# A graph-network layer on one core: the first and the second matmul layer of an edge group in two alternating halves

## The chip, the core and the metric

The kernel runs on one core of a Trainium2 chip. The core has a matrix engine (TensorE; PE in the profile, with its weight loads as PEld), a vector engine (DVE), a scalar engine (ACT), a general engine (POOL), an engine that issues transfers (SP), and 16 DMA engines. The metric is the device time of one execution in microseconds. A group of numbers such as 128x256 is partitions by elements.

## The reference

There are 6250 nodes with 128 features and 100000 edges, sorted by destination. The part that takes the time is the edge network, whose messages are summed by destination:

```python
row, col = (edge_index[0], edge_index[1])
msg_in = jnp.concatenate([node_features[row], node_features[col]], axis=-1)
h = jax.nn.relu(msg_in @ Wm1 + bm1)
h = jax.nn.relu(h @ Wm2 + bm2)
messages = h @ Wm3 + bm3
agg = jax.ops.segment_sum(messages, col, num_segments=num_nodes)
count = jax.ops.segment_sum(jnp.ones((messages.shape[0],), messages.dtype), col, num_segments=num_nodes)
agg = agg / jnp.clip(count, 1.0)[:, None]
node_in = jnp.concatenate([node_features, agg], axis=-1)
upd = jax.nn.relu(node_in @ Wn1 + bn1) @ Wn2 + bn2
return node_features + upd
```

Outside it, the result is `_layernorm(x + that)`. Hidden width is 256, so a hidden vector is two chunks of 128 (`HC = 2`).

## The kernel before, in words

**Tables.** `Wm1` is split into its half for the source and its half for the destination. A first stage computes a table `atab` with one row of 256 numbers in f32 for each node (the source's share of the first layer), and a table `btab` with the destination's share, each number as three bf16 terms. Later blocks of `btab` are made inside the edge loop (L663, then `b_terms`).

**The edge loop.** Edges go in 196 groups of 512 (`NG`, `GT = 4` tiles of 128 edges). The source rows of a group are gathered from `atab` by four indirect DMAs of 128 rows each, issued by POOL (L455), into one buffer `rows`, of which a pool holds four. The destination terms of a group come by two DMAs (groups 0 to 107, `nk` = 1) or four (groups 108 to 195, `nk` = 2) that SP issues (L466), into `terms`, six buffers. Then for group g:

- `first_layer` builds the first layer's sums in one PSUM tile `ph` of two banks, one bank for each half of the partitions (`h`), and both chunks `c` in each bank. Sixteen transposes (L509) bring the gathered rows into it; bf16 matmuls (L516), four of 256 columns with `nk` = 1 and eight of 128 columns with `nk` = 2, add the destination's terms. Two ACT instructions of 128x512 (L521) add the bias, apply relu, and write `h1` in SBUF.
- `second_layer` of group g-1 follows: for two pairs of tiles, a PSUM bank with four f32 matmuls of 256 columns (each is two matmul instructions in the profile, so eight a bank and sixteen a group, L530); one DVE instruction of 128x512 (L532) a bank takes it to `h2`.
- Before the second layer, in some groups, `sums` (L542) adds up edges by destination with one-hot matmuls, ACT copies the result (L550), and at the start of the next group TensorE turns it (L561) and DVE adds it to the totals (L571). Up to group 83 four groups are added at a time, then two, and from group 160 on one.

The first six groups (`XS = 3`) gather from `x` itself and use a matmul (L504) in place of the transposes.

**Order.** TensorE, ACT and DVE run in the order in which the program is written (the manual schedule). In an iteration that is on TensorE: turning of old sums, `first_layer(g)`, sums, `second_layer(g - 1)`, and sometimes a block of `btab`. POOL and SP keep a planner's order; their instructions wait for semaphores. A `rows` buffer comes free when all sixteen transposes that read it are done; the gathers of group g+4 wait for that. There are two `ph` tiles, so a group's first layer may begin while the previous group's is still being read.

**After the loop** a node stage of some 100 us computes the update and the layer norm. A further loop over groups with a wide range of destinations (L694) stands in the program and calls the same two functions, with a run-time count.

Of the kernel before, what the change touches and what calls it, by code (L numbers as in the profile page):

```python
# [33 lines left out]
def kernel(  # L34
# [181 lines left out]
            nc.sync.dma_start(btab[n0:n0 + (i + m) * P].rearrange("(p i) c h -> p i c h", p=P), bt[:, :i + m])  # L216

    edge = ExitStack()
    ld = edge.enter_context(tc.tile_pool(name="ld", bufs=4, side="right"))

    with tc.tile_pool(name="prep", bufs=1) as prep, tc.tile_pool(name="pp", bufs=3, space=PSUM) as pp, tc.tile_pool(
        name="pb", bufs=5, space=PSUM
# [181 lines left out]
        b_block = None  # L404
        for i in range(BLOCKS):
            tiles = range(4 * i, min(4 * i + 4, NT), 2)
            rows = ld.tile([P, GT, H], F32, name="rows")
# [29 lines left out]
    with edge, tc.tile_pool(name="wk", bufs=2) as wk, tc.tile_pool(  # L437
# [8 lines left out]
        def bank():  # L446
            return p2.tile([P, 2, H], F32, name="bank")
# [1 line left out]
        def flat_bank():  # L449
            return bank().rearrange("p t h -> p (t h)")  # L450

        def gather(idx):
            ag = ld.tile([P, GT, H], F32, name="rows")
            for j in range(GT):
                nc.gpsimd.indirect_dma_start(  # L455
                    out=ag[:, j, :], out_offset=None, in_=atab[:, :],
                    in_offset=bass.IndirectOffsetOnAxis(ap=idx[:, j:j + 1], axis=0))
            return ag
# [3 lines left out]
        def fetch(firsts, nk):  # L462
            bw = ld.tile([P, 2, H], BF16, name="terms", bufs=6)
            for j in range(0, len(firsts), 2 // nk):
                terms = btab[ds(firsts[j], WB + 1)].rearrange("n c h -> (n c) h")
                nc.sync.dma_start(bw[halves[j // 2], j % 2, :], terms[:NQ])  # L466
            return bw
# [27 lines left out]
            (nc.scalar.copy if g % 2 else nc.vector.tensor_copy)(xt, px)  # L495
            return xt

        def first_layer(ag, bw, oht, nt, nk, xt=None):
            nh = nt // 2
            ph = p1.tile([P, 2, HC, HE], F32, name="ph")  # L500
            for c in range(HC):
                if xt is not None:
                    for h in range(nh):
                        nc.tensor.matmul(ph[:, h, c, :], w1[:, 0, c * P:(c + 1) * P], xt[:, h * HE:(h + 1) * HE],  # L504
                                         start=(c == 0), stop=False, skip_group_check=True)
                    continue
                for u in range(GT):
                    for h in range(nh):
                        nc.tensor.matmul(ph[:, h, c, u * NQ:(u + 1) * NQ], ag[halves[h], u, c * P:(c + 1) * P],  # L509
                                         ident[halves[h], halves[h]], is_transpose=True,  # L510
                                         start=(c == 0 and u == 0), stop=False, skip_group_check=True)
            n = HE // nk
            for c in range(HC):
                for k in range(nk):
                    for h in range(nh):
                        nc.tensor.matmul(ph[:, h, c, k * n:(k + 1) * n], bw[halves[h], k, c * P:(c + 1) * P],  # L516
                                         oht[halves[h], k * n:(k + 1) * n], start=False, stop=True,
                                         skip_group_check=True)
            h1 = wk.tile([P, HC, GE], F32, name="h1", bufs=3)
            for c in range(HC):  # L520
                nc.scalar.activation(h1[:, c, :nh * HE].rearrange("p (h e) -> p h e", h=nh), ph[:, :nh, c, :],  # L521
                                     AF.Relu, bias=b1[:, c:c + 1])
            return h1

        def second_layer(h1, h2, nt):
            for j0 in range(0, nt, 2):
                ph2 = bank()
                for j in range(j0, j0 + 2):
                    for c in range(HC):
                        nc.tensor.matmul(ph2[:, j - j0, :], h1[:, c, j * P:(j + 1) * P],  # L530
                                         w2[:, c, :], start=(c == 0), stop=(c == HC - 1))
                nc.vector.tensor_tensor(h2[:, j0:j0 + 2, :H], ph2, nb2.to_broadcast([P, 2, H]), op=ALU.max)  # L532

        def sums(banks):

# [48 lines left out]
        def nk_of(g):  # L584
            return 1 if g < 2 * HALVES else 2
# [33 lines left out]
        for i in range(NG + 2 + WAIT + 1):  # L619
# [10 lines left out]
            if i < NG:  # L630
                bw = fetch(load_bases(tilei[0:1, i * GT:(i + 1) * GT], NTS[i], ENG.SP), nk_of(i))
                if i % 4 == 0 and i + 4 < NG:
                    rels[i // 4 + 1] = places(i // 4 + 1)
                st[i] = dict(bw=bw, ag=gather(srcT[:, i, :]) if i >= 2 * XS else None)
            g = i - 2
            if g < 0:
                continue
# [4 lines left out]
                turning = None  # L642
            if g < NG:
                s = st[g]
                s["h1"] = first_layer(s.pop("ag"), s.pop("bw"), ohts[g // 2][:, g % 2], NTS[g], nk_of(g),
                                      xts.pop(g, None))
                if g + 1 < 2 * XS:
                    xts[g + 1] = x_turn(g + 1)
                if g % 2 == 0 and g + 2 < NG:
                    make_hot(g // 2 + 1)  # L650
            if g in jobs:
                gs = jobs.pop(g)
                units_now = [w for k in gs for w in units_of(k)]
# [40 lines left out]
        with tc.For_i(0, groups, 1) as g:  # L694
            more = nc.values_load(
                morei[0:1, ds(g, 1)], min_val=0, max_val=N // 16,
                skip_runtime_bounds_check_because="the difference of two nodes over 16")
            dcol = wk.tile([P, GT], I32, name="dcol", bufs=1)
            bcol = wk.tile([P, GT], F32, name="bcol", bufs=1)
            dl = wk.tile([P, GT], F32, name="dl", bufs=1)  # L700
            db = wk.tile([P, HE], I32, name="db", bufs=1)
            with nc.allow_non_contiguous_dma(reason="a destination a partition"):
                nc.sync.dma_start(dcol, dpad[ds(g * GE, GE)].rearrange("(j p) -> p j", p=P))
            for h, half in enumerate(halves):
                nc.sync.dma_start(db[half], dpad_row[:, ds(g * GE + h * HE, HE)].to_broadcast([NQ, HE]))
            nc.sync.dma_start(bcol, basetab.rearrange("(o t) -> o t", o=1)[:, ds(g * GT, GT)].to_broadcast([P, GT]))
            nc.vector.tensor_sub(dl, dcol, bcol)
            with tc.For_i(0, more, 1):
                idx = wk.tile([P, GT], I32, name="idx")
                nc.vector.tensor_copy(idx, srcT[:, ds(g, 1), :].rearrange("p o j -> p (o j)"))  # L710
                pbc = wk.tile([P, 2], F32, name="pbc")
                for h, half in enumerate(halves):
                    nc.vector.tensor_scalar(pbc[half], bcol[half, 2 * h:2 * h + 2], iota_p[half], None, op0=ALU.add)

                ti = wk.tile([1, GT], I32, name="ti")
                nc.vector.tensor_scalar_min(ti, tilei[0:1, ds(g * GT, GT)], float(N - 1))
                ag, bw = gather(idx), fetch(load_bases(ti, GT, ENG.SP), 2)
# [5 lines left out]
                h1 = first_layer(ag, bw, oht[:, 0], GT, 2)  # L723
                second_layer(h1, h2s[0], GT)
# [186 lines left out]
```

## Time and profile before

| | |
|---|---|
| median of 3 runs | 1420.95 us (1420.75 to 1423.0) |
| the profiled execution | 1419.83 us, span 1418.1 us |
| TensorE busy | 1254.4 us, 88% of the span, 10152 matmuls |
| POOL busy | 766.0 us, 54% (760 gathers in the edge loop) |
| DVE busy | 535.5 us, 38% |
| ACT busy | 374.8 us, 26% |
| DMA | 165.66 MB, 117 GB/s on average |
| mean granted TensorE clock | 0.968 of full |

How to read it. In the list of groups a row gives line, engine, operation, what is written and read, its shape, how often, then busy time and the mean of one, then the idle time just before these instructions and what ended it. "issue" there means that the engine waited for nothing that the profile shows. In the timeline a row gives the start, the time from the first start to the last end of the merged instructions, the engine, the line, the operation, the count, and in brackets the idle time before it. A matmul's stated duration is longer than the step from one to the next, as they are pipelined: steps are read from starts. Instruction counts in the text count a weight load and a matmul as two.

### The profile page before, as it was taken

Reading aid. Unit: us, or ns where it says so; the run is one execution under the profiler, and the core shown is the slowest. Engines: PE = TensorE matmul, PEld = TensorE weight load, DVE = VectorE, ACT = ScalarE, POOL = GpSimd, SP = SyncE. Lnnn points to the kernel's source line nnn. Section 1 sums busy time; section 2 is a strip of 40 time slices with the busy share of each in tenths; the row PEclk is TensorE's granted clock in tenths of the full one; section 3 lists DMA queues with packets and bytes.
Section 4 is the critical chain, followed back from the end, with each engine's and each line's share of the span. In section 5 each row is a group of like instructions: output and inputs, shape, how many; then the busy total and the mean of one; then the engine's idle time right before and its main releaser. Section 6 shows DMA issues by size and latency. Waiting matters only on the chain. (4 is left out here: it accounts for less than half of the span.)

```text
span 1418.1 us, 27156 instructions
## 1 busy us (share of the span) xinstructions
PE 1254.4 (88%) x10152; PEld 921.6 (65%) x10153; DVE 535.5 (38%) x1289; ACT 374.8 (26%) x674; POOL 766.0 (54%) x810
## 2 busy tenths in 40 slices
PE   4689899898988988898988888998989889999997
PEld 3566676676666766676766666676666666667555
DVE  2533333333333423333333333333333344444554
ACT  1442222222222222222222122222222222222234
POOL 6125566565665655656656566566666656652210
PEclk8789999999999999999999999999999999999999
DMA  6533244344344434434334443444444444441422
GB/s 220 201 92 106 80 146 127 96 135 124 115 120 119 126 103 126 130 99 140 111 111 115 118 119 113 123 116 120 113 119 119 113 123 113 113 114 31 114 79 74
DMA packets 106276, 165.66 MB, mean 117 GB/s; under 512 B 26443, under 2 KB 66633, under 8 KB 106125
## 3 DMA queue, kind: packets, MB, share of 16 engines
q0 software_dynamic: 37248, 101.24, 25.7%
q1 hardware_dynamic: 68349, 62.39, 14.2%
q8 instruction: 81, 1.33, 0.4%
q14 instruction: 54, 0.44, 0.1%
q10 hardware_dynamic: 544, 0.26, 0.1%
HBM read 144.27 MB, written 19.89 MB: 116 GB/s over the span
## 5 line engine op out<-in xcount | busy, mean ns | idle before, releaser
L455 POOL DMA_INDIRECT rows<-atab,srcT x760 | 723.5, 952 | 528.5 <-PE ph L516 228.3
L530 PE MATMUL bank<-w,h 128*128 128x256 f32 x3128 | 746.1, 390 | 11.0 <-issue 8.8
L530 PEld LDWEIGHTS bank<-w,h 128*128 128x128 f32 x3128 | 585.8, 193 | 154.2 <-issue 64.2
L521 ACT ACTIVATE h<-ph,b 128x512 f32<-128x512 f32 x392 | 247.3, 682 | 733.8 <-PE ph L516 419.0
L532 DVE TENSOR_TENSOR x_sb<-bank,nb 128x512 f32<-128x512 f32 x313 | 214.3, 691 | 568.5 <-PE bank L530 224.1
L542 PE MATMUL bank<-x_sb,oh 128*32 128x257 f32 x1252 | 135.4, 402 | 22.7 <-issue 21.7
L516 PE MATMUL ph<-oht,terms 64*128 64x128 bf16 (+1 forms) x1132 | 97.0, 240 | 52.8 <-issue 45.4
L509 PE MATMUL ph<-ident,rows 64*128 64x64 f32 x3032 | 133.2, 227 | 3.3 <-issue 3.3
L509 PEld LDWEIGHTS ph<-ident,rows 64*128 64x128 f32 x3032 | 111.2, 139 | 36.0 <-issue 36.0
L532 DVE TENSOR_TENSOR h_more<-bank,nb 128x512 f32<-128x512 f32 x78 | 53.4, 691 | 148.6 <-PE bank L530 70.1
L571 DVE TENSOR_TENSOR acc<-acc,bank 128x96 f32 x378 | 96.1, 254 | 23.0 <-PE ph L516 2.4
L542 PEld LDWEIGHTS bank<-x_sb,oh 128*32 128x32 f32 x1252 | 51.6, 112 | 70.1 <-issue 53.9
L516 PEld LDWEIGHTS <-terms 64*128 64x128 bf16 x1132 | 46.9, 97 | 69.9 <-issue 62.3
L542 PE MATMUL bank<-h_more,oh 128*32 128x257 f32 x312 | 63.0, 407 | 5.1 <-issue 4.7
L550 ACT COPY part<-bank 128x257 f32<-128x257 f32 (+1 forms) x95 | 35.6, 374 | 110.0 <-PE bank L530 59.3
L792 POOL TENSOR_TENSOR agg<-agg,rc 128x512 f32<-128x512 f32 (+2 forms) x15 | 18.5, 1238 | 85.2 <-DVE agg L790 45.6
L561 PEld LDWEIGHTS bank<-ident,part 64*128 64x128 f32 x567 | 25.1, 138 | 55.0 <-ACT part L550 27.6
L561 PE MATMUL bank<-ident,part 64*128 64x64 f32 x567 | 38.3, 240 | 22.5 <-ACT part L550 21.5
L370 PE MATMUL pbt<-w,xT 128*128 128x256 f32 x114 | 32.1, 430 | 18.4 <-ACT xT L389 10.8
L484 DVE TENSOR_TENSOR oh<-iota_n,dloc 128x256 f32<-128x256 f32 x98 | 41.0, 418 | 0.0
L370 PEld LDWEIGHTS pbt<-w,xT 128*128 128x128 f32 x114 | 23.3, 217 | 22.7 <-ACT xT L389 11.6
L479 DVE TENSOR_SCALAR oht<-places,iota_p 128x512 bf16<-128x512 bf16 x98 | 33.7, 344 | 0.0
(138 smaller groups left out, 537.0 us busy)
## 6 DMA issues: line engine op xcount, KB each, us to landing
terms<-btab SPq DMA_DIRECT2D x566, 32.0 KB
places<-reltab SPq DMA_DIRECT2D x98, 128.0 KB
rows<-atab,srcT POOLq DMA_INDIRECT x760
btab<-x_sb SPq DMA_DIRECT2D x10, 768.0 KB
atab<-rows SPq DMA_DIRECT2D x12, 512.0 KB
x_sb<-in_x_dram SPq DMA_DIRECT2D x5, 512.0 KB
xr<-in_x_dram SPq DMA_DIRECT2D x10, 256.0 KB
rc<-rtab SPq DMA_DIRECT2D x10, 256.0 KB
```

Source lines behind the costliest of these rows:

```text
L370: nc.tensor.matmul(pbt[:, a, :], xT[:, (t0 + a) * P:(t0 + a + 1) * P], w1[:, k, :], start=True, stop=True)
L455: nc.gpsimd.indirect_dma_start(out=ag[:, j, :], out_offset=None, in_=atab[:, :], in_offset=bass.IndirectOffsetOnAxis(ap=idx[:, j:j + 1], a ...
L484: nc.vector.tensor_tensor(oh[:, :ng].rearrange("p g j n -> p (g j) n"), iota.to_broadcast([P, ng * GT, WN]), dl.rearrange("p (j o) -> p j ...
L509: nc.tensor.matmul(ph[:, h, c, u * NQ:(u + 1) * NQ], ag[halves[h], u, c * P:(c + 1) * P], ident[halves[h], halves[h]], is_transpose=True, ...
L516: nc.tensor.matmul(ph[:, h, c, k * n:(k + 1) * n], bw[halves[h], k, c * P:(c + 1) * P], oht[halves[h], k * n:(k + 1) * n], start=False, st ...
L521: nc.scalar.activation(h1[:, c, :nh * HE].rearrange("p (h e) -> p h e", h=nh), ph[:, :nh, c, :], AF.Relu, bias=b1[:, c:c + 1])
L530: nc.tensor.matmul(ph2[:, j - j0, :], h1[:, c, j * P:(j + 1) * P], w2[:, c, :], start=(c == 0), stop=(c == HC - 1))
L532: nc.vector.tensor_tensor(h2[:, j0:j0 + 2, :H], ph2, nb2.to_broadcast([P, 2, H]), op=ALU.max)
L542: nc.tensor.matmul(pg[w * WN:(w + 1) * WN, :H + 1], oh, h2, start=(t == 0), stop=(t == len(tiles) - 1), skip_group_check=True)
L550: nc.scalar.copy(part[:nt * WN, i], pg[:nt * WN, :H + 1])
L561: nc.tensor.matmul(pts[h][:, i, c, :], rows, ident[halves[h], halves[h]], is_transpose=True, start=True, stop=True, skip_group_check=True)
L571: nc.vector.tensor_add(window, window, pts[h][:, i, :, k:k + WN])
```

## The change

A group's first layer is cut in two halves `s` = 0, 1. Half 0 transposes the rows of gathers 0 and 1, half 1 those of gathers 2 and 3; each adds its destination terms and has ACT instructions of its own, on 128x256 in place of 128x512. Every half has four bf16 matmuls of 128 columns, for both values of `nk`. The second layer is cut by edge tiles in the same way (tiles 0 and 2, then 1 and 3; one PSUM bank and one DVE instruction each, as before). In an iteration TensorE now runs: turning of old sums, first layer of g half 0, sums, second layer of g-1 half 0, first layer of g half 1, second layer of g-1 half 1. The four `rows` buffers are one tile, addressed by `g % 4`, so that a gather waits for the readers of its own part. The wide loop's calls change along.

```diff
-    ld = edge.enter_context(tc.tile_pool(name="ld", bufs=4, side="right"))
+    ld = edge.enter_context(tc.tile_pool(name="ld", bufs=1, side="right"))
+    rows_of_groups = ld.tile([P, 4, GT, H], F32, name="rows")
...
-        def gather(idx):
-            ag = ld.tile([P, GT, H], F32, name="rows")
+        def gather(g, idx):
+            ag = rows_of_groups[:, g % 4]
...
-        def first_layer(ag, bw, oht, nt, nk, xt=None):
+        def first_layer(part, s):
+
+            ag, bw, oht, nt, nk, xt = part["of"]
             nh = nt // 2
-            ph = p1.tile([P, 2, HC, HE], F32, name="ph")
+            if s == 0:
+                part["ph"] = p1.tile([P, 2, HC, HE], F32, name="ph")
+                part["h1"] = wk.tile([P, HC, GE], F32, name="h1", bufs=3)
+            ph, h1 = part["ph"], part["h1"]
             for c in range(HC):
...
-                for u in range(GT):
+                for u in (2 * s, 2 * s + 1):
                     for h in range(nh):
...
-            n = HE // nk
+            k = s if nk == 2 else 0
             for c in range(HC):
-                for k in range(nk):
-                    for h in range(nh):
-                        nc.tensor.matmul(ph[:, h, c, k * n:(k + 1) * n], bw[halves[h], k, c * P:(c + 1) * P],
-                                         oht[halves[h], k * n:(k + 1) * n], start=False, stop=True,
-                                         skip_group_check=True)
-            h1 = wk.tile([P, HC, GE], F32, name="h1", bufs=3)
+                for h in range(nh):
+                    nc.tensor.matmul(ph[:, h, c, s * P:(s + 1) * P], bw[halves[h], k, c * P:(c + 1) * P],
+                                     oht[halves[h], s * P:(s + 1) * P], start=False, stop=True,
+                                     skip_group_check=True)
             for c in range(HC):
-                nc.scalar.activation(h1[:, c, :nh * HE].rearrange("p (h e) -> p h e", h=nh), ph[:, :nh, c, :],
-                                     AF.Relu, bias=b1[:, c:c + 1])
-            return h1
+                nc.scalar.activation(h1[:, c, :].rearrange("p (h s e) -> p h s e", h=2, s=2)[:, :nh, s],
+                                     ph[:, :nh, c, s * P:(s + 1) * P], AF.Relu, bias=b1[:, c:c + 1])
...
+        def second_layer(h1, h2, nt, s):
+            js = range(s, nt, 2)
+            ph2 = bank()
+            for i, j in enumerate(js):
+                for c in range(HC):
+                    nc.tensor.matmul(ph2[:, i, :], h1[:, c, j * P:(j + 1) * P],
+                                     w2[:, c, :], start=(c == 0), stop=(c == HC - 1))
+            m = len(js)
+            nc.vector.tensor_tensor(h2[:, s:s + 2 * m - 1:2, :H], ph2[:, :m], nb2.to_broadcast([P, m, H]), op=ALU.max)
...
-                s["h1"] = first_layer(s.pop("ag"), s.pop("bw"), ohts[g // 2][:, g % 2], NTS[g], nk_of(g),
-                                      xts.pop(g, None))
+                s["of"] = s.pop("ag"), s.pop("bw"), ohts[g // 2][:, g % 2], NTS[g], nk_of(g), xts.pop(g, None)
+                first_layer(s, 0)
...
-            if 0 <= g - 1 < NG:
-                second_layer(st.pop(g - 1)["h1"], h2s[(g - 1) % len(h2s)], NTS[g - 1])
+            for half in range(2):
+                if half and g < NG:
+                    first_layer(st[g], 1)
+                if 0 <= g - 1 < NG:
+                    second_layer(st[g - 1]["h1"], h2s[(g - 1) % len(h2s)], NTS[g - 1], half)
+            st.pop(g - 1, None)
```

More of the change, by code (lines that the diff above doesn't have):

```diff
@@ L406 @@
             tiles = range(4 * i, min(4 * i + 4, NT), 2)
-            rows = ld.tile([P, GT, H], F32, name="rows")
+            rows = rows_of_groups[:, i % 4]
             for n, t0 in enumerate(tiles):
@@ L496, in x_turn @@
             return xt
-        def first_layer(ag, bw, oht, nt, nk, xt=None):
+        def first_layer(part, s):
+            ag, bw, oht, nt, nk, xt = part["of"]
             nh = nt // 2
-            ph = p1.tile([P, 2, HC, HE], F32, name="ph")
+            if s == 0:
+                part["ph"] = p1.tile([P, 2, HC, HE], F32, name="ph")
+                part["h1"] = wk.tile([P, HC, GE], F32, name="h1", bufs=3)
+            ph, h1 = part["ph"], part["h1"]
             for c in range(HC):
                 if xt is not None:
-                    for h in range(nh):
+                    for h in range(nh if s == 0 else 0):
                         nc.tensor.matmul(ph[:, h, c, :], w1[:, 0, c * P:(c + 1) * P], xt[:, h * HE:(h + 1) * HE],
@@ L511, in first_layer @@
                                          start=(c == 0 and u == 0), stop=False, skip_group_check=True)
-            n = HE // nk
+            k = s if nk == 2 else 0
             for c in range(HC):
-                for k in range(nk):
-                    for h in range(nh):
-                        nc.tensor.matmul(ph[:, h, c, k * n:(k + 1) * n], bw[halves[h], k, c * P:(c + 1) * P],
-                                         oht[halves[h], k * n:(k + 1) * n], start=False, stop=True,
-                                         skip_group_check=True)
-            h1 = wk.tile([P, HC, GE], F32, name="h1", bufs=3)
-            for c in range(HC):
-                nc.scalar.activation(h1[:, c, :nh * HE].rearrange("p (h e) -> p h e", h=nh), ph[:, :nh, c, :],
-                                     AF.Relu, bias=b1[:, c:c + 1])
-            return h1
[L525 to L532, printed above, removed]
+                for h in range(nh):
+                    nc.tensor.matmul(ph[:, h, c, s * P:(s + 1) * P], bw[halves[h], k, c * P:(c + 1) * P],
+                                     oht[halves[h], s * P:(s + 1) * P], start=False, stop=True,
+                                     skip_group_check=True)
+            for c in range(HC):
+                nc.scalar.activation(h1[:, c, :].rearrange("p (h s e) -> p h s e", h=2, s=2)[:, :nh, s],
[9 more added lines that the diff above has]
+            nc.vector.tensor_tensor(h2[:, s:s + 2 * m - 1:2, :H], ph2[:, :m], nb2.to_broadcast([P, m, H]), op=ALU.max)
         def sums(banks):
@@ L633 @@
                     rels[i // 4 + 1] = places(i // 4 + 1)
-                st[i] = dict(bw=bw, ag=gather(srcT[:, i, :]) if i >= 2 * XS else None)
+                st[i] = dict(bw=bw, ag=gather(i, srcT[:, i, :]) if i >= 2 * XS else None)
             g = i - 2
@@ L716 @@
                 nc.vector.tensor_scalar_min(ti, tilei[0:1, ds(g * GT, GT)], float(N - 1))
-                ag, bw = gather(idx), fetch(load_bases(ti, GT, ENG.SP), 2)
+                ag, bw = gather(0, idx), fetch(load_bases(ti, GT, ENG.SP), 2)
                 oht = wk.tile([P, 2, HE], BF16, name="oht")
@@ L722 @@
                 oh = hot_nodes(dl, 1, iota_b)
-                h1 = first_layer(ag, bw, oht[:, 0], GT, 2)
-                second_layer(h1, h2s[0], GT)
+                wide = dict(of=(ag, bw, oht[:, 0], GT, 2, None))
+                for half in range(2):
+                    first_layer(wide, half)
+                for half in range(2):
+                    second_layer(wide["h1"], h2s[0], GT, half)
                 part = part_of(sums([[[(oh[:, 0, j, :], h2s[0][:, j, :])] for j in range(GT)]]), [GT])
```

## The prediction, made before the result was known

> **What bounds the kernel now.** I read the page first, then busy time by stage, then the timeline of TensorE in groups with and without idle time, then the waits.
>
> The page's busy times, and three stretches of the loop (columns: stretch, its length, busy time and count of PE, PEld, DVE, ACT and POOL, granted clock, DMA share, GB/s):
>
> ```profile
> PE 1254.4 (88%) x10152; PEld 921.6 (65%) x10153; DVE 535.5 (38%) x1289; ACT 374.8 (26%) x674; POOL 766.0 (54%) x810
> ```
> ```profile
> 618.00:1098.00 480.00, 432.61 (x3856) 320.18 (x3854) 171.71 (x402) 114.22 (x199) 293.60 (x310) 0.99 0.42 118
> 1098.00:1275.00 177.00, 159.38 (x1542) 117.18 (x1540) 72.78 (x192) 42.93 (x84) 107.20 (x114) 1.00 0.41 115
> 1286.00:1303.00 17.00, 17.00 (x186) 12.95 (x180) 8.66 (x24) 4.95 (x10) 0.63 (x1) 1.00 0.08 17
> ```
>
> TensorE is the bound, yet in most of the loop it idles for a tenth; at 1286 to 1303, when gathers and destination terms are over (DMA share 0.08), it does not idle at all. The same groups with and without idle time:
>
> ```profile
> 1161.62 0.66 PE L509 MATMUL ph<-ident,rows 64*128 64x64 f32 x16
> 1162.12 0.57 PE L516 MATMUL ph<-oht,terms 64*128 64x128 bf16 x4
> 1163.20 0.29 PE L516 MATMUL ph<-oht,terms 64*128 64x128 bf16 x4 [0.51 <-issue]
> ...
> 1167.88 0.66 PE L509 MATMUL ph<-ident,rows 64*128 64x64 f32 x16
> ```
> ```profile
> 1285.91 0.66 PE L509 MATMUL ph<-ident,rows 64*128 64x64 f32 x16
> 1286.41 0.39 PE L516 MATMUL ph<-oht,terms 64*128 64x128 bf16 x8
> 1286.73 0.64 PE L542 MATMUL bank<-h_more,oh 128*32 128x257 f32 x8
> ...
> 1291.18 0.66 PE L509 MATMUL ph<-ident,rows 64*128 64x64 f32 x16
> ...
> 1296.45 0.66 PE L509 MATMUL ph<-ident,rows 64*128 64x64 f32 x16
> ```
>
> A group takes 6.26 us (1161.62 to 1167.88) or 5.27 (1285.91 to 1291.18). The lost microsecond lies inside the bf16 matmuls, at the end of a run of small instructions, and waits for nothing that the profile shows. In the waits of TensorE such "issue" leads:
>
> ```profile
> PE ph L516 <- issue: 45.4, 74, 1.5
> PE bank L542 <- issue: 26.4, 53, 1.1
> PE bank L561 <- ACT part L550: 21.5, 12, 5.0
> ```
>
> What the loop loses in all comes from paces. Starts of the transposes, from group 6 on, with groups of a full pace between them:
>
> ```profile
> 113.58 0.71 PE L509 MATMUL ph<-ident,rows 64*128 64x64 f32 x16
> ...
> 120.20 0.66 PE L509 MATMUL ph<-ident,rows 64*128 64x64 f32 x16
> ...
> 403.90 0.66 PE L509 MATMUL ph<-ident,rows 64*128 64x64 f32 x16
> ...
> 409.23 0.71 PE L509 MATMUL ph<-ident,rows 64*128 64x64 f32 x16
> ...
> 413.74 0.71 PE L509 MATMUL ph<-ident,rows 64*128 64x64 f32 x16
> ...
> 623.68 0.71 PE L509 MATMUL ph<-ident,rows 64*128 64x64 f32 x16
> ...
> 906.66 0.66 PE L509 MATMUL ph<-ident,rows 64*128 64x64 f32 x16
> 911.13 0.71 PE L509 MATMUL ph<-ident,rows 64*128 64x64 f32 x16
> ...
> 926.17 0.71 PE L509 MATMUL ph<-ident,rows 64*128 64x64 f32 x16
> ...
> 931.92 0.66 PE L509 MATMUL ph<-ident,rows 64*128 64x64 f32 x16
> ...
> 1098.27 0.71 PE L509 MATMUL ph<-ident,rows 64*128 64x64 f32 x16
> ```
>
> Groups 6 to 85 go in fours: one with sums, 6.62 (113.58 to 120.20), one with a block of `btab`, 5.33 (403.90 to 409.23), two plain ones at 4.51 (409.23 to 413.74): 20.97. Twenty fours are 419; they took 510 (113.58 to 623.68). Groups 86 to 161 go in pairs of 5.75 (926.17) and 4.47 (906.66): 38 pairs are 388, and took 475 (to 1098.27). Groups 162 to 193 at 5.27 are 169, and took 198 (to 1296.45). The loss is 91 + 87 + 29 = 207 us, over twice the idle time that the page books, since a stated matmul duration covers part of each gap. This is what the change could win; it adds no speed elsewhere.
>
> **The change part by part.** *Twice as many switches.* Now TensorE goes once a group from the f32 matmuls of the second layer (128 rows) to the transposes and bf16 matmuls (64 rows) and back, then twice. A switch has a price:
>
> ```profile
> 518.11 0.71 PE L509 MATMUL ph<-ident,rows 64*128 64x64 f32 x16
> ...
> 518.66 0.38 PE L516 MATMUL ph<-oht,terms 64*128 64x256 bf16 x4
> 518.97 3.72 PE L530 MATMUL bank<-w,h 128*128 128x256 f32 x16
> 520.43 1.26 ACT L521 ACTIVATE h<-ph,b 128x512 f32<-128x512 f32 x2 [3.60 <-PE ph L516]
> 522.62 0.71 PE L509 MATMUL ph<-ident,rows 64*128 64x64 f32 x16
> ```
> ```profile
> 389.77 2.75 PE L530 MATMUL bank<-w,h 128*128 128x256 f32 x12
> ```
> ```profile
> 1284.72 1.03 PE L530 MATMUL bank<-w,h 128*128 128x256 f32 x4
> ```
>
> Twelve matmuls within a run take 2.75 and four 1.03, so a step is (2.75 - 1.03) / 8 = 0.215, and sixteen are 3.44. From the first of sixteen to the next transposes it is 3.65 (518.97 to 522.62): 0.21 for going in and out. The small ones take 0.55 + 0.31 = 0.86 where their steps give some 0.70 (sixteen transposes to the first bf16 matmul 0.50 at 1285.91, and eight bf16 in 0.39 against four in 0.29 at 1163.20, 0.025 each). A round trip costs 0.21 at least and 0.37 at most. I take 0.35, near the whole, as the second trip repeats each edge of the first. For 190 groups with transposes that is 66 us of TensorE's own time; nothing hides it where TensorE never rests, and where it rests it may fall into the gap (a rival).
>
> *Bf16 matmuls.* In 108 groups four of 256 columns become eight of 128: 432 matmuls and 432 loads more. The four take 0.31 (518.66 to 518.97), the eight 0.32 (1286.41 to 1286.73): nothing, in either direction up to 1 us in all. [...]
>
> *A new wait.* Both halves of the first layer lie in the same two banks. TensorE's half 1 therefore has to wait until ACT has read half 0, with the second layer's half 1 and all of the next group queued behind it in TensorE's order. No row of before shows this wait. [...] The price:
>
> ```profile
> L521 ACT ACTIVATE h<-ph,b 128x512 f32<-128x512 f32 x390 | 246.4, 683 | 730.1 <-PE ph L516 415.3 <-remote 214.9 <-PE bank L530 71.0
> ...
> L806 ACT ACTIVATE u<-put,bu 128x256 f32<-128x256 f32 x8 | 3.8, 473 | 8.4 <-PE put L805 8.4
> ```
>
> Two halves of 0.473, overlapped a little as now (2 x 0.683 in 1.26), are 0.85. The cover is eight matmuls, 1.83 with the first one's delay, plus sums. So TensorE waits only if ACT starts over some 0.9 us late. It often does: the bf16 matmuls above end at 518.66 + 0.38 = 519.04 and ACT starts at 520.43, 1.39 later, with nothing else on it. Over 0.9 that is 0.5. In groups with sums the cover is 0.6 to 1.9 longer. I take 0.5 for a plain group in four and in two, some 30 times: 15 us. Bounds: 0 if signals come at once, and 0.5 for all 190 groups, 95 us.
>
> *Shorter runs.* Between f32 matmuls there were up to 48 small instructions (60 with L561), plus sums; now 24 (36). Sums still follow half 0, so a run with them goes from 80 to 56 or from 104 to 88. I let the whole 45.4 us of L516 go, and half of the 26.4 at L542: 59 us less. Bounds: nothing, if the gaps come from outside TensorE's stream; twice as much and more, 117 us, if the hidden part of the gaps goes too (207 against 102 booked).
>
> *Buffers by halves.* Gathers are never late: L509 has no wait for a DMA above, and four buffers hold four groups. Earlier release alone wins nothing. POOL now waits twice a group:
>
> ```profile
> L455 POOL DMA_INDIRECT rows<-atab,srcT x760 | 723.5, 952 | 528.5 <-PE ph L516 228.3 <-issue 178.4 <-remote 60.6
> ```
>
> It rests for over a microsecond a group already; four gathers take about 5 us of 6.2 (723.5 us busy and 178.4 between them for 760 make 1.19 each, 4.7 a group). Cost zero while TensorE's group stays above 5; without that cover a late gather would show on L509. SP's fetch waits for the last bf16 matmul of a group, now half a group later; six buffers cover it.
>
> *ACT and DVE.* Four instructions of 0.473 for two of 0.683 add 0.53 a group, 103 us, on an engine with 26% busy: nothing beyond the wait above. DVE does the same work; its writes to `h2` are only spaced.
>
> *Sum.* 1419.8 + 66 + 15 - 59 = 1442, against the profiled execution; the median lies 1.1 us above it, within the spread of the runs. A difference under 0.2%, 2.8 us, can't be told from none.
>
> **The rivals.** *Shorter runs win (faster).* If the idle time comes from the length of a run, its hidden part goes too: 1420 + 66 - 117 = 1369, and with all 207 gone 1279. It decides against me as soon as more than 66 + 15 = 81 of the 207 us go. For it: the gap sits at the end of the longest run of small instructions. Against: at 1285.91 the very same run has no gap, so its length isn't enough; the DMA traffic has to be there, and that stays.
>
> *The new wait bites (slower still).* If TensorE's signals stay late everywhere and no idle time goes: 1420 + 66 + 15 = 1501, and to 1580 with the upper bound. For it: ACT's 1.39. Against: after a gap signals come at once, so gap and wait replace each other.
>
> *The gap swallows the cost (no change).* Groups of 108 and fewer instructions all go at near 6.2 while DMA runs. If traffic sets that pace, 66 us fall into the gap: 1420. Against: plain groups run at 4.51 in the same traffic.
>
> **How the numbers follow.** The sum's case 0.41, the wait 0.13, shorter runs 0.40, swallowed 0.06. The likeliest gives 1442, its own range 1425 to 1475 (relief of 30 to 75 us). From 1365 to 1505 leaves out the far ends of both rivals, some 2 in 10. Faster 0.41, same 0.04, slower 0.55.
>
> **What would show it.** Right: two visits of L530 with eight matmuls each and a plain group without gaps at 4.86; "issue" before L516 nearly gone and before L542 halved; a wait of L509 for ACT L521, at some 15 us; gathers never waited for. Wrong: the loop's pace nearer to 5.6 a group after 1098 (shorter runs), or L509 waiting for ACT in most groups, or a wait of L509 for gathers, if one tile in place of four makes them wait for more than their own part.

## The result, and the profile after

The changed kernel takes 1442.29 us (median, 1436.87 to 1446.0), the kernel before beside it 1420.85. The ratio is 1.0146, with a 95% interval of 1.0108 to 1.0185: slower by 1.5%. The forecast was 1442.

One thing has to be known to read the numbers below: in one set of runs the kernel before took 1208.6 us in place of 1420 to 1432, with the same transfers and, to judge by its time and by the traces of the other kernels of that set, with almost none of its loop's idle time, so each ratio here is taken only against the kernel before of its own set.

The profiled execution of the changed kernel took 1436.87 us, with a span of 1435.1. First its page, in the rows that answer to those shown of before. Line numbers have moved: transposes are L515, bf16 matmuls L521, ACT's first layer L525, second layer L533, sums L546, ACT's copy of the sums L554, turning L565, gathers L456.

```profile
PE 1270.2 (89%) x10584; PEld 904.1 (63%) x10585; DVE 536.8 (37%) x1290; ACT 456.3 (32%) x1066; POOL 764.4 (53%) x810
...
L456 POOL DMA_INDIRECT rows<-atab,srcT x760 | 721.8, 950 | 545.3 <-PE ph L521 212.1
...
L525 ACT ACTIVATE h<-ph,b 128x256 f32<-128x256 f32 (+1 forms) x784 | 328.6, 470 | 712.3 <-PE ph L521 320.0
```

What TensorE waited for (engine, tile, line, what ended the wait: us in all, times, longest):

```profile
PE ph L515 <- issue: 51.5, 53, 2.4
PE ph L515 <- ACT h L525: 31.5, 29, 3.4
PE bank L533 <- issue: 19.9, 26, 1.7
...
PE bank L546 <- issue: 5.4, 12, 1.0
...
PE bank L565 <- ACT part L554: 1.1, 2, 0.6
PE ph L521 <- issue: 0.8, 2, 0.5
```

The three places that led before are nearly empty: the bf16 matmuls went from 45.4 to 0.8, the sums from 26.4 to 5.4, turning from 21.5 to 1.1. A new place stands in for them: the transposes of half 1, with 31.5 us put down to ACT and 51.5 to nothing. They are one place: of these 83 us, 81 (77 waits) end within 0.15 us of the end of ACT's instructions on half 0, however they are booked. In the timeline (start, time, engine, line, operation, idle time before) ACT begins half 0 at 789.78 and ends at 790.62, and the transposes, booked as "issue", begin 0.05 later:

```profile
787.38 0.27 PE L521 MATMUL ph<-oht,terms 64*128 64x128 bf16 x4
...
787.58 1.99 PE L533 MATMUL bank<-w,h 128*128 128x256 f32 x8
...
787.97 0.95 POOL L456 DMA_INDIRECT rows<-atab,srcT  x1 [0.31 <-issue]
789.78 0.84 ACT L525 ACTIVATE h<-ph,b 128x256 f32<-128x256 f32 x2 [2.35 <-PE bank L533]
789.81 0.69 DVE L536 TENSOR_TENSOR x_sb<-bank,nb 128x512 f32<-128x512 f32 x1 [1.01 <-PE bank L533]
789.85 0.95 POOL L456 DMA_INDIRECT rows<-atab,srcT  x1 [0.93 <-PE bank L533]
...
790.67 0.46 PE L515 MATMUL ph<-ident,rows 64*128 64x64 f32 x8 [1.09 <-issue]
```

The bf16 matmuls of half 0 ended at 787.65, so ACT was 2.13 us late. DVE and POOL, which wait for other signals of TensorE, started within 0.07 us of it (DVE's matmuls had ended shortly before, at 789.57; POOL had been idle since 788.92). The booked idle time of all these places is as large as before: 110 us, against 105 (45.4, 26.4 and 21.5, with 8.8 at the second layer and 3.3 at the transposes). So whatever idle time the change wins back isn't in what the page books; it is worked out further down. A plain group without a gap shows the new order, two visits to the second layer with eight matmuls each:

```profile
165.14 0.46 PE L515 MATMUL ph<-ident,rows 64*128 64x64 f32 x8
165.43 0.28 PE L521 MATMUL ph<-oht,terms 64*128 64x128 bf16 x4
165.64 1.99 PE L533 MATMUL bank<-w,h 128*128 128x256 f32 x8
167.56 0.47 PE L515 MATMUL ph<-ident,rows 64*128 64x64 f32 x8
167.86 0.28 PE L521 MATMUL ph<-oht,terms 64*128 64x128 bf16 x4
168.07 1.99 PE L533 MATMUL bank<-w,h 128*128 128x256 f32 x8
170.00 0.46 PE L515 MATMUL ph<-ident,rows 64*128 64x64 f32 x8
```

From 165.14 to 170.00 are 4.86 us; before, it was 4.51.

### The profile page after: what moved, and what is told of

Read it like the earlier page. It is cut to its first block, busy times and chain, and to the rows that moved or that the text cites. A ratio compares the mean times of both kernels' runs of the same rounds, so it can differ in the third digit from the quotient of the medians.

```text
span 1435.1 us, 29213 instructions
## 1 busy us (share of the span) xinstructions
PE 1270.2 (89%) x10584; PEld 904.1 (63%) x10585; DVE 536.8 (37%) x1290; ACT 456.3 (32%) x1066; POOL 764.4 (53%) x810
## 3 DMA queue, kind: packets, MB, share of 16 engines
q8 instruction: 85, 1.39, 0.4%
## 5 line engine op out<-in xcount | busy, mean ns | idle before, releaser
L456 POOL DMA_INDIRECT rows<-atab,srcT x760 | 721.8, 950 | 545.3 <-PE ph L521 212.1
L533 PE MATMUL bank<-w,h 128*128 128x256 f32 x3128 | 792.3, 395 | 22.6 <-issue 19.9
L533 PEld LDWEIGHTS bank<-w,h 128*128 128x128 f32 x3128 | 566.4, 191 | 162.1 <-issue 48.6
L525 ACT ACTIVATE h<-ph,b 128x256 f32<-128x256 f32 (+1 forms) x784 | 328.6, 470 | 712.3 <-PE ph L521 320.0
L515 PE MATMUL ph<-ident,rows 64*128 64x64 f32 x3032 | 173.3, 233 | 84.8 <-issue 51.5
L515 PEld LDWEIGHTS ph<-ident,rows 64*128 64x128 f32 x3032 | 125.1, 139 | 188.6 <-issue 139.2
L546 PE MATMUL bank<-x_sb,oh 128*32 128x257 f32 x1252 | 109.2, 386 | 4.4 <-issue 4.3
L521 PE MATMUL ph<-oht,terms 64*128 64x128 bf16 x1564 | 110.6, 218 | 1.4 <-issue 0.8
L521 PEld LDWEIGHTS <-terms 64*128 64x128 bf16 x1564 | 63.3, 98 | 7.3 <-issue 6.2
L554 ACT COPY part<-bank 128x257 f32<-128x257 f32 (+1 forms) x95 | 35.7, 375 | 92.5 <-PE ph L515 26.0
L546 PEld LDWEIGHTS bank<-x_sb,oh 128*32 128x32 f32 x1252 | 42.3, 109 | 30.0 <-issue 8.8
L546 PE MATMUL bank<-h_more,oh 128*32 128x257 f32 x312 | 53.9, 390 | 1.2 <-issue 1.1
L565 PEld LDWEIGHTS bank<-ident,part 64*128 64x128 f32 x567 | 24.8, 137 | 33.0 <-issue 30.2
L565 PE MATMUL bank<-ident,part 64*128 64x64 f32 x567 | 38.0, 239 | 1.1 <-ACT part L554 1.1
```

What stands on the lines that cost most here:

```text
L456: nc.gpsimd.indirect_dma_start(out=ag[:, j, :], out_offset=None, in_=atab[:, :], in_offset=bass.IndirectOffsetOnAxis(ap=idx[:, j:j + 1], a ...
L521: nc.tensor.matmul(ph[:, h, c, s * P:(s + 1) * P], bw[halves[h], k, c * P:(c + 1) * P], oht[halves[h], s * P:(s + 1) * P], start=False, st ...
L525: nc.scalar.activation(h1[:, c, :].rearrange("p (h s e) -> p h s e", h=2, s=2)[:, :nh, s], ph[:, :nh, c, s * P:(s + 1) * P], AF.Relu, bias ...
L533: nc.tensor.matmul(ph2[:, i, :], h1[:, c, j * P:(j + 1) * P], w2[:, c, :], start=(c == 0), stop=(c == HC - 1))
L546: nc.tensor.matmul(pg[w * WN:(w + 1) * WN, :H + 1], oh, h2, start=(t == 0), stop=(t == len(tiles) - 1), skip_group_check=True)
L554: nc.scalar.copy(part[:nt * WN, i], pg[:nt * WN, :H + 1])
```

## The experiments

My theory was the sum: TensorE's own switches cost some 66 us, and the shorter runs give less than that back. Against it stood that the new wait alone makes the change slow, and that the extra instructions do.

### Both orders without the gathers and the destination terms

```diff
+                if i < 6 or 108 <= i < 114:
+                    bw = fetch(...)
+                    bws[i % 6] = bw
+                bw = bws[i % 6]
...
+                if 2 * XS <= i < 2 * XS + 4:
+                    ags[i % 4] = gather(...)
+                st[i] = dict(bw=bw, ag=ags[i % 4] if i >= 2 * XS else None)
```

The kernel before:

> The kernel before with nearly all gathers and nearly all transfers of destination terms in the edge loop left out (the four row buffers and six term buffers are filled a first time and then used again; the output is not the reference's). If TensorE's idle time in the loop comes with that DMA traffic, the 207 us that the loop loses against its full pace go: about 1213 (1200 to 1235). If it comes from the long runs of small instructions alone, the time stays above 1380.

The changed kernel:

> The changed kernel with the same gathers and transfers left out as in the kernel before without them (the output is not the reference's). What it is longer than that one is the price of the new order without gaps: by the sum's switches 66 us (40 to 71) if ACT's half 0 is always done in time, so 1279 beside 1213; 0 to 10 if switches are free and only late signals make the change slow; over 100 if half 1's transposes wait for ACT even without the traffic.

Measured: 1220.47 us (1220.17 and 1220.78), and 1294.62 (1293.92 and 1295.31); the kernel before, whole, took 1423.81 beside them. Busy time by stage of the kernel before without the transfers:

```profile
618.00:1098.00 480.00, 480.00 (x4821) 374.11 (x4820) 217.49 (x538) 133.99 (x249) 0.00 (x0) 1.00 0.05 15
```

TensorE does not rest at all in this stretch, where it was busy for 432.61 of 480. So the 207 us that were worked out from paces are there: 1420.9 - 1220.5 = 200. Plain groups of the two kernels, the kernel before first:

```profile
149.60 0.71 PE L509 MATMUL ph<-ident,rows 64*128 64x64 f32 x16
...
154.11 0.71 PE L509 MATMUL ph<-ident,rows 64*128 64x64 f32 x16
```
```profile
155.40 0.46 PE L515 MATMUL ph<-ident,rows 64*128 64x64 f32 x8 [0.36 <-ACT h L525]
...
157.83 0.46 PE L515 MATMUL ph<-ident,rows 64*128 64x64 f32 x8
...
162.69 0.46 PE L515 MATMUL ph<-ident,rows 64*128 64x64 f32 x8
```

4.51 against 4.86 (157.83 to 162.69). The new order costs 74.2 us where nothing is late: 190 groups by 0.35 are 66, and the wait for ACT that is left even here is 6.9 in all, some 0.36 in the groups where ACT also takes a block of `btab` (the first row). By the same difference the changed kernel loses 1442.3 - 1294.6 = 148 us to the transfers, where the kernel before loses 200: a relief of 53.

### Half 1 with PSUM banks of its own

```diff
-            if s == 0:
+            if s == 0 or xt is None:
                 part["ph"] = p1.tile([P, 2, HC, HE], F32, name="ph")
+            at = s * P if xt is not None else 0
...
-                                         start=(c == 0 and u == 0), stop=False, skip_group_check=True)
+                                         start=(c == 0 and u == 2 * s), stop=False, skip_group_check=True)
...
-                                     ph[:, :nh, c, s * P:(s + 1) * P], AF.Relu, bias=b1[:, c:c + 1])
+                                     ph[:, :nh, c, at:at + P], AF.Relu, bias=b1[:, c:c + 1])
```

> The changed kernel, but each half of a group's first layer has a PSUM tile of its own, so that TensorE's half 1 no longer has to wait until ACT has read half 0. The changed kernel idles 31.5 us in front of half 1's transposes with ACT booked and 51.5 us at the same place with nothing booked, 83 together. Theory W (the wait on the shared banks makes the change slow, the price of the switches is small): these 83 us go, 1442 - 83 = 1359, faster than before. Theory S (TensorE's own switches make it slow, as in the sum with 66 us; the idle time only moves to another place when the wait is taken away, since signals and instructions are late for a reason outside TensorE): 1427 to 1442, the 'issue' before the second layer or the sums grows by about what the wait loses. Below 1380 speaks for W, above 1420 for S.

Measured: 1441.03 us beside 1423.81, ratio 1.0118 (1.0089 to 1.0147). The wait is gone and nothing is won. Its largest waits of TensorE (L535 is the second layer, L548 the sums):

```profile
PE bank L535 <- issue: 47.3, 84, 1.9
PE bank L548 <- issue: 16.4, 33, 1.1
```

The transposes wait 2.8 us in all now, and the second layer and the sums took the idle time over (47.3 from 19.9, 16.4 from 5.4); of the 80 us, some 38 come back there as booked idle time. The page's busy time of TensorE rose from 1270.2 to 1300.4, too, for the same instructions, so that gaps lie inside stated durations. The time is that of theory S: the wait is where the lateness shows, not its source.

### Both halves in a row

```diff
                 first_layer(s, 0)
+                first_layer(s, 1)
...
-                if half and g < NG:
-                    first_layer(st[g], 1)
```

This stands on the kernel with own banks, so it also has the rows freed by parts.

> As the run with own banks, but both halves of the first layer stand in a row, and the second layer is whole after them: all new instructions (432 more bf16 matmuls, four ACT instructions for two) without the alternation. Theory S: the extra instructions cost nothing, the switches are gone again, so the kernel before's time, 1421, within 8 us. [...] If ACT's four shorter instructions hurt by themselves (signals to and from ACT), 1430 to 1470. Theory W says nothing of it beyond 1421.

Measured: 1472.47 beside 1423.81, ratio 1.0339 (1.0289 to 1.0388). A miss for my theory, by 48 us. To see whose time that is, the same without the transfers:

> The kernel with both halves of the first layer in a row, without nearly all gathers and transfers of terms (the output is not the reference's). With the traffic it was 51 us slower than the kernel before. If its extra instructions cost nothing of TensorE's own time, 1220 as the kernel before without the traffic (1215 to 1228), and the 51 us come from the traffic's hold on the supply of instructions or signals. [...]

Measured: 1204.66 beside 1208.57, in the set without idle time. Its groups 6 to 86 take 5.24 each, from the starts of the transposes, where the kernel before without transfers takes 5.23; groups 108 to 160 take 5.12 in both. The 432 extra matmuls and ACT's halves cost nothing by themselves: 0.01 a group by these paces, with four matmuls more in each. So the 48 us come only with the transfers and the idle time (in what way, no run shows), and the one part not yet looked at by itself is the buffers.

### The buffers alone, and the alternation alone

```diff
+    rows_of_groups = ld.tile([P, 4, GT, H], F32, name="rows")
...
-            ag = ld.tile([P, GT, H], F32, name="rows")
+            ag = rows_of_groups[:, g % 4]
```

> The kernel before with one part of the change alone: the four row buffers are one tile addressed by group, so that each gather waits for the readers of its own part. The order of the layers is that of before. Expected no difference: within 4 us of the kernel before beside it (1421, or 1209 if it has no idle time), since no transposes wait for a gather. Rival: the one tile makes gathers or transposes wait for more than their own part, slower by 10 us or more, with a wait of the transposes for the gather's DMA.

> The changed kernel once more, beside the kernel before. In the runs with two groups a switch the kernel before took 1209 us in place of 1421, with the same transfers and without TensorE's idle time. Theory S (the change costs 66 to 74 us of TensorE's own time, and in the first comparison 200 us of idle time gave 53 of them back): if the kernel before is at 1209 here, the changed one is at 1275 to 1290, slower by 5 to 7%; if it is at 1421, the changed one is again at 1437 to 1446. Theory T (a cost of 1.5% whatever the idle time): 1227 beside 1209.

Measured in one set, where the kernel before took 1432.44: the buffers alone 1487.43, ratio 1.0378 (1.0340 to 1.0415); the whole change 1464.06, ratio 1.0198 (1.0162 to 1.0235). The buffers alone are the slower by 55 us. The transposes wait for no gather; the idle time lies at TensorE's own instructions and at ACT's copy of the sums (L510 transposes, L543 sums, L562 turning):

```profile
PE ph L510 <- issue: 51.8, 79, 1.3
PE bank L543 <- issue: 33.3, 73, 1.8
PE bank L562 <- ACT part L551: 30.2, 23, 3.0
```

Neither of the two expectations had this. What the buffers do change is on POOL: every gather now waits by itself, with 784 waiting instructions on POOL in the trace where there were 227. The 48 us of the halves in a row may be these 55: the intervals of the two ratios overlap, though the runs are of different sets. Then the change with the old buffers:

```diff
-    rows_of_groups = ld.tile([P, 4, GT, H], F32, name="rows")
...
-            ag = rows_of_groups[:, g % 4]
+            ag = ld.tile([P, GT, H], F32, name="rows")
```

> The changed kernel with the buffers of before: four whole row buffers, whose four gathers together wait once for a group's transposes, in place of one tile by parts, where each gather waits by itself. So the alternation alone. With the buffers alone the kernel was 55 us slower (1487 beside 1432), with both parts 32 us slower (1464). Theory A (the two parts add, the gathers' own waits are what costs in the buffers): 1464 - 55 = 1409 beside 1432, faster than before. Theory S (the alternation costs by itself what the whole change cost; the buffers' 55 us come in only where the runs of small instructions are long): 1440 to 1465. If the kernel before has no idle time here (1209), the alternation shows its own price with all transfers: 1275 to 1290.

Measured: 1533.68 beside 1420.22, ratio 1.0819 (1.0776 to 1.0863). Neither theory: the alternation alone costs 113 us, and with the buffers by parts 21 to 32. The parts don't add; the buffers cost 55 in the old order and win 82 to 92 in the new one. The new wait is what bites here:

```profile
PE ph L514 <- ACT h L524: 164.6, 89, 3.6
```

The timeline of one such wait (POOL's gathers L455, half 0's bf16 matmuls L520, ACT L524):

```profile
911.60 0.94 POOL L455 DMA_INDIRECT rows<-atab,srcT  x1 [1.38 <-PE ph L520]
...
912.85 0.95 POOL L455 DMA_INDIRECT rows<-atab,srcT  x1 [0.31 <-issue]
...
913.43 0.28 PE L520 MATMUL ph<-oht,terms 64*128 64x128 bf16 x4
...
914.11 0.95 POOL L455 DMA_INDIRECT rows<-atab,srcT  x1 [0.32 <-issue]
...
915.37 0.95 POOL L455 DMA_INDIRECT rows<-atab,srcT  x1 [0.30 <-issue]
...
917.42 0.84 ACT L524 ACTIVATE h<-ph,b 128x256 f32<-128x256 f32 x2 [5.08 <-remote]
```

The bf16 matmuls end at 913.71; ACT, with nothing to do, starts at 917.42, 3.71 later and 1.1 after the last of four gathers in a row ended (916.32). It is not the only one: between 130 and 1060 us, over the ACT instructions that open a half with ACT idle, those over 2 us late start, by their median, 1.12 us after the end of the last gather here (45 of them) and 1.23 in the changed kernel (59). What differs is the string: with whole buffers the four gathers of a group come as one (135 of 141 strings in that stretch, a string ending where POOL rests for over 0.5), with parts as two (105 strings) or four (84). The tenth of the ACT instructions that is latest is over 3.65 us late with whole buffers and over 2.19 with parts. In these two kernels longer strings of gathers and later signals go together; that the one holds the other up is only argued. In the set without idle time two groups a switch had strings of up to 352 gathers and no late signal. POOL's next gather waits for a signal of TensorE as well (280 times in the changed kernel, by the list of waits; the row at 789.85 above is one), so a late signal may also be what ends a string. And length alone doesn't decide it: with strings of four in the old order, the latest tenth is over 2.87 us late in the kernel before and over 5.06 with the buffers alone. Why the buffers by parts hurt in the old order, where the strings are mostly four long with either buffer, stays open.

### Which transfers, and fewer switches

Two kernels left out the gathers alone and the terms alone:

> The kernel before without nearly all gathers of the edge loop, the transfers of destination terms kept (the output is not the reference's). Without both it took 1220.5, with both about 1422. If the gathers alone make TensorE's idle time, about 1225; if the terms alone, above 1380; if both share it, in between: 1290 to 1340.

> The kernel before without nearly all transfers of destination terms, the gathers kept (the output is not the reference's). If the gathers alone make TensorE's idle time, above 1400; if the terms alone, about 1225; if both share it, 1290 to 1340.

They took 1196.79 and 1193.91, ratios 0.9901 (0.9864 to 0.9938) and 0.9877 (0.9842 to 0.9912), but in the set without idle time, where the kernel before itself took 1208.57 with all transfers. So they can't tell which transfers count; and the set shows that the transfers alone don't make the idle time. Nor is the loop the only place where it differs: group 6 starts some 90 us into these two executions, where it started at 117.6 in the first kernel without transfers; that one, at 1220, took longer than the kernel with all transfers here. In the same set ran the order with fewer switches:

```diff
+            paired = 2 * XS + 2 <= g < 2 * PAIRS
+            if g < NG and not (paired and g % 2):
+                for k in ((g, g + 1) if paired else (g,)):
+                    ... first_layer of group k
...
+            for k in () if paired and g % 2 else (g - 1, g) if paired else (g - 1,):
+                ... second_layer of group k
```

> The kernel before, but from group 8 to 159 the first layers of two groups stand in a row, and the second layers of two groups after them: 76 round trips between small and large matmuls fewer. Theory S (the switches cost 0.35 to 0.39 each, also under the traffic): 27 to 30 us less, 1393. Theory T (under the traffic the loop goes at 6.2 to 6.4 us a group whatever TensorE's own time is, as both the kernel before and the changed one did in groups 6 to 107): within 8 us of 1421. Theory L (the idle time grows with the length of a run of small instructions): 1440 to 1470.

Measured: 1199.68 beside 1208.57, ratio 0.9935 (0.9913 to 0.9957). Its stage in pairs:

```profile
841.21 0.39 PE L561 MATMUL bank<-ident,part 64*128 64x64 f32 x6
841.44 0.66 PE L509 MATMUL ph<-ident,rows 64*128 64x64 f32 x16
...
842.16 0.66 PE L509 MATMUL ph<-ident,rows 64*128 64x64 f32 x16
...
851.32 0.66 PE L509 MATMUL ph<-ident,rows 64*128 64x64 f32 x16
```

A pair takes 9.88 (841.44 to 851.32) where it took 10.22 without gaps: one round trip fewer, 0.34 us less. That is the price of a switch from the other side. Not all of the expected 27 to 30 came, since in the stage in fours an undisturbed four takes 20.60 in place of 20.96, and late terms cost a part (its mean there is 5.40 a group, where the kernels without gathers and without terms take 5.26 and 5.23):

```profile
PE ph L516 <- DMA terms<-btab: 12.8, 18, 1.4
```

With eight buffers of terms:

> Two groups a switch, as before, with eight buffers of destination terms in place of six. With six, the bf16 matmuls waited 12.8 us for the terms' DMA, which the kernel before doesn't show in such a quantity. Theory S: this wait goes, and the fewer switches win 20 to 30 us in all, 1180 to 1190 beside 1209 (or 1391 to 1401 beside 1421, if the idle time is there and doesn't grow). If the wait comes from SP's order and not from the buffers: 1200 beside 1209.

Measured: 1709.02, but now in a set with idle time, beside 1432.44: ratio 1.1900 (1.1854 to 1.1945). Its largest waits:

```profile
PE bank L530 <- issue: 158.5, 231, 1.8
PE bank L530 <- ACT part L550: 50.1, 19, 8.8
```

A group of 108 to 160 takes 8.93 us where the same order took 4.94 in the other set. Runs of small instructions are twice as long here, and strings are of eight gathers (57 of 59); the kernel takes 277 us more than the kernel before of its set, and some 500 more than nearly the same order in the other set (1709 against 1200). A part of this is TensorE's granted clock, in the pages' rows (a digit for a fortieth of the span, in tenths of full speed; this kernel first, then two groups a switch with six buffers):

```profile
PEclk8799988898898889888878788888888899999999
```
```profile
PEclk9899999999999999999999999999999999998999
```

The trace has the clock at half for 362 us of this loop, which at half speed is some 181 us of work lost (an estimate), against 6.8 us of the other loop. Run length and string length go together in this kernel and aren't told apart, and the two buffers more are in it as well. No kernel here that moves all the data beat the kernel before in the sets with idle time; in the one without, two groups a switch did by 0.65%.

## Why the prediction was right, point by point

**The loss in the loop** (207 us from paces): 200 without the transfers. Right, in size too.

**Switches** (0.35 us a group, 66 us): 4.86 and 4.51 a plain group, 74.2 us without transfers, of which 6.9 are a wait for ACT; and 0.34 in the pairs with one switch fewer. Right.

**Bf16 matmuls and ACT's extra time** (nothing): 5.24 and 5.23 a group without the transfers. Right; two halves of ACT take 0.84 (forecast 0.85).

**The new wait** (15 us): mis-sized. It is 83 us with the "issue" at the same place, and 164.6 with whole buffers, over the upper bound of 95. The step that failed is the count of late starts and their size: I took 30 of 0.5, from a lag of 1.39 seen once, and there are 82 waits of 1.0 on average. But as the kernel with own banks shows, its net price is nil (1441 without it, 1442 with it), as the idle time goes elsewhere without it.

**Shorter runs** (59 us less): mis-sized the same way round. The places named lost 86 us of booked idle time (45.4 to 0.8, 26.4 to 5.4, and turning, which I hadn't counted, 21.5 to 1.1). Relief and wait together were forecast at 59 - 15 = 44 and are 53 (the medians of the kernels with and without transfers). But the booked idle time as a whole didn't fall (105 and 110), so the 53 lie in what the page doesn't book: of the loss to the transfers, 200 - 105 = 95 before and 148 - 103 = 45 now (6.9 of the 110 stand without the transfers too). Some 12 us of this difference of 50 are, as an estimate, the granted clock: it is half of full for 47.8 us of the loop before and for 23.9 of the changed one; the prediction put all of the hidden part down to gaps under stated durations. With the wait at 83, the relief is 83 + 53 = 136, beyond the upper bound of 117. The two errors cancel, and so the sum, 1420.9 + 74.2 - 52.7 = 1442.4, comes out at the forecast. That shorter runs are the cause of the relief isn't shown either: the alternation with whole buffers has the same short runs and costs 113, 39 more than the 74 of the new order without transfers, so that it has no net relief at all. Right in the sum, in part by luck.

**Buffers by halves** (nothing, cost zero): wrong, and in the step that seemed safest. That gathers are never late was right (no wait of the transposes for a gather's DMA stands in the list of before, of after or of the buffers alone). But I asked only whether the transposes wait for them. The buffers also set when the gathers are issued, and in what strings, and they lost 55 us in the old order and won 82 to 92 in the new, more than the whole net relief of 53; in what way isn't shown. POOL doesn't wait twice a group either, but before each gather. Here, too, the term that I left out stands inside the relief that I did forecast.

**The rivals.** "Shorter runs win" needed more relief than switches and wait cost together, 81 us by the prediction and 74 + 83 = 157 as measured, and got 136. "The new wait bites" (1501 to 1580) is what the alternation does with whole buffers, 1534; the buffers by parts are what keeps the change out of it. "The gap swallows the cost" is nearer than its 0.06 told: with all transfers the two kernels go at 6.38 and 6.39 us a group in groups 6 to 86, and the 10 us by which the loop of the profiled execution is longer come from groups 108 on; 6 more lie ahead of group 6.

## What to carry to other kernels

Price a reordering twice: in the engine's own time, which paces of undisturbed groups gave here to some ten per cent (66 for 74), and in what the idle time does, which could here only be bounded. A part of a change that "hides" may still set when another engine's string of transfers starts; test it alone and left out, since two such parts need not add (here 55 us and 113 alone, 21 to 32 together). And run the kernel before beside every variant: an order that won 0.65% in one set lost 19%, with two buffers more, in another.

## What the runs showed of the hardware

In these runs ACT, though idle, started up to microseconds after the matmuls that it waited for. With the idle time present, half of its opening instructions that found it idle started over 1.53 us, and a tenth over 2.87, after the last bf16 matmul in the kernel before (126 between 130 and 1060 us; in the 39 from there to 1300 us the median is 0.16). Where a gap lay inside the group's bf16 matmuls, ACT followed after 0.15 (median of 62 in the whole loop), elsewhere after 1.68 (107): gap and lag replace each other, as the prediction said. In the set without idle time, the same instructions (in the order with two groups a switch) started 0.04 us after, at most 0.39, with more bytes a second moving (134 GB/s against 118 in the same stretch):

```profile
618.00:1098.00 480.00, 476.20 (x4788) 378.67 (x4787) 228.05 (x559) 128.60 (x247) 334.16 (x354) 0.99 0.48 134
```

What makes the difference lies outside the program: the kernel before took 1423.81 and 1208.57 us in two sets, both on the chip that the record numbers 11. No run here names it.

The granted clock was lower in the runs with idle time. The trace notes it as full or as half. Without the transfers its mean is 1.00 from 113 to 1098 us in both kernels; in the loop of the kernel before it is half in 11 stretches of 3.4 or 6.8 us, 47.8 in all. Inside them the second layer's matmuls start 0.427 us apart, elsewhere 0.216 (medians). Whether the gaps bring the half clock, or both have one cause, no run here separates.
